# A bottleneck pair on one core: first loads and products in another order, and the last convolutions' seven products moved into the common PSUM pool

## The chip, the cores and the metric

One Trainium2 chip, one of its cores. The metric is the device time of one execution in microseconds (us). The kernel before took 2366.21 us, the median of 4 runs from 2364.62 to 2367.03.

## What is computed

Two residual blocks in a row on x, 16 images of 1024 channels by 32x32 pixels, all in float32:

```python
# layer 0: a bottleneck with local self-attention
h = relu(bn(conv1x1(x, w_conv1)))            # 1024 -> 256
q, k, v = relu(bn(h*wq)), relu(bn(h*wk)), bn(h*wv)
# 3x3 neighbourhoods of k (plus a position table), 32 heads of 8 channels, softmax over 9 taps
h = relu(bn(softmax(q . unfold(k)) . unfold(v)))
x = relu(bn(conv1x1(h, w_conv3)) + x)        # 256 -> 1024
# layer 1: an ordinary bottleneck
h = relu(bn(conv1x1(x, w1)))                 # 1024 -> 256
h = relu(bn(conv3x3(h, w2)))                 # 256 -> 256
x = relu(bn(conv1x1(h, w3)) + x)             # 256 -> 1024
```

## The kernel before, in words

**Tiling.** Channels lie on the 128 partitions, the 1024 pixels of an image on the free axis. A PSUM tile is 128x1024 (two banks of 512); one product is a matmul of 128x128 weights with 128x512 pixels. In float32 the profile shows each product as two MATMUL rows.

**Stages.** The list `stages` names, image by image, the work of TensorE (PE): `conv1` (`first_conv`, L390 through `reduce_part`), `qk` and `v` (`project`, L476, with the position products L522), `fused` (conv3 of layer 0, L422, followed by conv1 of layer 1, L390), `wino` (the 3x3 convolution of four images at once in a Winograd form, `winograd_conv`, L823) and `u3` (the last 1x1 convolution, L422 in `last_sum`). For the last four images (12 to 15) the last convolution is done in another way, `late_sums`: outputs and inputs are split in halves, and a Strassen-like scheme takes seven products in place of eight. `late_weights` makes sums of weights, `change(b)` makes four sums of the image's halves on VectorE (DVE, L1213 to L1220), and a `Pair` handles two output channel blocks with products 1 to 7 (L1252).

**What sets the order.** Nothing is scheduled automatically: the program is written in the order in which each engine runs it, and semaphores hold an instruction until its data and its room are there. The DVE and ScalarE (ACT) work of attention, transforms and weights is drawn into the PE stages word by word from the string `ORDER` (L916): after each part of a stage `Side.passes` takes a word, and its letters run one step of attention (`j`), of its exponentials (`e`), of transforms and weights (`f`), of relays (`m`), ReLU of attended images (`a`), or ReLU of a Winograd image (`w`).

**The start.** `at_first` (L1434) issues loads. `more_weights` (L113) puts weights on SP's DMA queue: the first half of `w1` in two pieces (128 KB, then 384 KB, L131). `more_loads` (L330, DMA at L362) puts x of image 0 on ACT's queue for chunks 0 (two halves) and 1 and on POOL's for chunks 2 to 7. Behind these POOL's queue runs `member_table` (L188, L190), clears `kp` (L1445) and loads the last convolutions' weights (L233). `winograd_weights` turns the 3x3 weights into 36 forms on ACT and DVE (L284 to L294) and writes them to `uw` in HBM (L306); its tiles come from `hpool`, five rooms that it shares with h, q and the attended images.

**The end.** Ahead of `late_sums` the pool `psum` (four 128x1024 tiles) is closed and a pool `banks` opened (four tags of two 128x512 banks). A `Pair` takes two residual tiles r. Its products 1, 6 and 5 add up in one bank, 7 and 4 in another, and DVE adds a bank into the residual in SBUF each time a partial sum is one of the outputs (L1241): 1 to the first half of r0, 6 and 4 to the first half of r1, 7 to the second half of r1, 5 to both second halves. Product 2 has a bank of its own and DVE adds it to r0. Product 3 has a bank into which ACT first copies the second half of r0 (L1237), and from which it copies the sum back (L1276). Then ACT makes both results (L1332: shift, ReLU, pixels put back in order) and POOL sends them (L1333). The last two pairs of image 15 go another way: residual copied to PSUM for both 2 and 3, results straight out of PSUM (L1329), and the very last one in quarters (L1298, L1304, L1305) with its output on SP's and ACT's queues.

## Time and profile before

| | |
|---|---|
| median of 4 runs | 2366.21 us |
| the profiled execution | 2365.78 us, of which the span is 2364.1 us |
| PE busy | 2347.7 us, 99% of the span |
| DVE, ACT, POOL busy | 91%, 39%, 21% |
| HBM traffic | 292 GB/s over the span |
| first product of PE starts | 4.39 us |
| step of two 128x512 MATMULs, all through | 0.43 us |
| last MATMUL starts | 2357.19 us |

PE's busy time is a union of rows that overlap, so "99%" says only that it rarely stood idle. To see a loss on PE one takes the step from one MATMUL's start to the next and compares it with the usual 0.43 us (0.22 us for 256 columns). Summed over the span these steps lose about 15 us; the largest single losses lie at the start, in two Winograd stages (at 678 and 2202 us), between `last_sum` and `late_sums` (2258 us), and at the very end.

### The profile page before, as it was taken

What the parts mean: (1) busy time and instruction counts of PE and PEld (TensorE: products, weight loads), DVE (VectorE), ACT (ScalarE), POOL (GpSimd) and SP (SyncE); (2) the same over time, 40 slices, a digit from 0 to 9 for tenths busy, and PEclk for the clock granted to TensorE, in tenths of its full rate; (3) what the DMA queues carried; (4) which work ended last, traced back from release to release, by engine and by line L of the source; (5) the groups of instructions that cost most, each with busy time, mean ns of one, the idle gap of its engine ahead of it and who ended that gap; (6) DMA issues with size and microseconds to landing.
All of it is one profiled execution on the core that took longest, in us unless ns stands there. A gap on an engine that the chain in (4) does not pass through costs nothing.

```text
span 2364.1 us, 18845 instructions
## 1 busy us (share of the span) xinstructions
PE 2347.7 (99%) x6244; PEld 1138.8 (48%) x6244; DVE 2163.1 (91%) x1786; ACT 931.7 (39%) x890; POOL 490.3 (21%) x900
## 2 busy tenths in 40 slices
PE   9999999999999999999999999999999999999998
PEld 3444444444475444444466444444467444444843
DVE  4999999999999999999989999999989999966687
ACT  3323342324123574433122574324222463444277
POOL 2212121212121332111121232111111231111222
PEclk9999999999999999999999999999999999999999
DMA  9968687978697997687887998688788897699887
GB/s 365 376 210 305 243 288 250 285 274 274 254 354 253 344 387 297 222 263 244 258 313 271 329 388 311 225 276 284 264 296 277 325 371 251 208 353 313 315 295 293
DMA packets 295585, 691.63 MB, mean 293 GB/s; under 512 B 20800, under 2 KB 165184, under 8 KB 286784
## 3 DMA queue, kind: packets, MB, share of 16 engines
q0 software_dynamic: 119888, 471.14, 54.5%
q1 hardware_dynamic: 174944, 218.06, 28.4%
q10 hardware_dynamic: 656, 1.23, 0.1%
q8 instruction: 50, 0.82, 0.1%
q14 instruction: 47, 0.39, 0.1%
HBM read 415.32 MB, written 275.03 MB: 292 GB/s over the span
## 4 chain that ended last, share of the span: by engine, by line
PE 95%; DMA 2%; DVE 2%; ACT 1%; issue 0%; SPq 0%; ACTq 0%; DVEq 0%
PE ps L390 36%; PE ps L422 32%; PE ps L476 13%; PE ps L823 9%; PE ps L1252 4%; DMA U<-uw 1%; DMA uw<-u 1%; DMA g<-in_u2t_dram 1%; PE ps L522 0%; DVE z L849 0%; DVE y L849 0%; ACT kp L489 0%; DVE prod L621 0%; DMA x<-in_x_dram 0%; DVE u L291 0%
## 5 line engine op out<-in xcount | busy, mean ns | idle before, releaser
L390 PE MATMUL ps<-result,u 128*128 128x512 f32 x1024 | 457.8, 592 | 0.0
L422 PE MATMUL ps<-a,w 128*128 128x512 f32 x1024 | 457.7, 592 | 0.0
L390 PE MATMUL ps<-x,w 128*128 128x512 f32 x1024 | 444.3, 594 | 4.5 <-DMA x<-in_x_dram 4.4
L678 DVE TENSOR_TENSOR acc<-e,bnv 128x2048 f32<-128x2048 f32 x144 | 327.5, 2283 | 18.5 <-ACT e L660 15.4
L422 PE MATMUL ps<-y,u 128*128 128x512 f32 x768 | 331.1, 592 | 0.0
L621 DVE TENSOR_TENSOR prod<-qc,bnk 128x2048 f32<-128x2048 f32 x144 | 324.1, 2287 | 1.8
L441 ACT ACTIVATE result<-ps,par 128x1024 f32<-128x1024 f32 x128 | 142.5, 1113 | 457.4 <-PE ps L422 394.0
L390 PEld LDWEIGHTS ps<-x,w 128*128 128x128 f32 x1024 | 195.1, 191 | 250.5 <-issue 242.8
L422 PEld LDWEIGHTS ps<-a,w 128*128 128x128 f32 x1024 | 194.6, 190 | 244.9 <-issue 243.7
L390 PEld LDWEIGHTS ps<-result,u 128*128 128x128 f32 x1024 | 194.4, 190 | 245.1 <-issue 237.8
L696 DVE TENSOR_TENSOR acc<-acc 128x2048 f32<-128x2048 f32 x128 | 293.4, 2292 | 4.4
L422 PEld LDWEIGHTS ps<-y,u 128*128 128x128 f32 x768 | 145.9, 190 | 183.3 <-issue 181.1
L476 PE MATMUL ps<-h,wqk 128*128 128x512 f32 x512 | 222.4, 592 | 0.3 <-ACT h L1091 0.3
L442 POOL DMA_DIRECT2D r<-result x128 | 68.7, 537 | 596.9 <-ACT result L441 592.7
L626 DVE TENSOR_TENSOR prod<-prod 128x2048 f32<-128x2048 f32 (+1 forms) x80 | 166.2, 2077 | 2.3
L476 PEld LDWEIGHTS ps<-h,wqk 128*128 128x128 f32 x512 | 97.1, 190 | 123.2 <-issue 111.2
L441 ACT ACTIVATE result<-ps,bn_sh 128x1024 f32<-128x1024 f32 x96 | 106.8, 1113 | 105.2 <-PE ps L422 102.6
L1091 ACT ACTIVATE h<-ps,par 128x1024 f32<-128x1024 f32 x32 | 38.4, 1203 | 259.7 <-PE ps L390 259.7
L413 ACT ACTIVATE ps<-s 128x1024 f32<-128x1024 f32 x128 | 131.2, 1025 | 15.7 <-DMA s<-in_x_dram 13.2
L489 ACT ACTIVATE kp<-ps,par 128x1024 f32<-128x1024 f32 x64 | 77.3, 1209 | 148.3 <-PE ps L476 116.2
L362 POOL DMA_DIRECT2D x<-in_x_dram x126 | 67.0, 533 | 275.7 <-PE ps L390 206.9
L846 ACT ACTIVATE z<-ps 128x1024 f32<-128x1024 f32 x48 | 49.2, 1024 | 178.7 <-PE ps L823 134.2
(384 smaller groups left out, 2675.3 us busy)
## 6 DMA issues: line engine op xcount, KB each, us to landing
s<-in_x_dram POOLq DMA_DIRECT2D x128, 512.0 KB, 5.9
r<-result POOLq DMA_DIRECT2D x128, 512.0 KB, 4.5
x<-in_x_dram POOLq DMA_DIRECT2D x126, 512.0 KB, 5.2
out_dram<-result POOLq DMA_DIRECT2D x125, 512.0 KB, 6.1
r<-r POOLq DMA_DIRECT2D x111, 512.0 KB, 6.9
v<-v SPq DMA_DIRECT2D x96, 408.0 KB, 4.9
U<-uw SPq DMA_DIRECT2D x60, 512.0 KB, 5.5
bnk<-kp SPq DMA_DIRECT2D x32, 680.0 KB, 7.2
```

What stands on the lines that cost most here:

```text
L390: nc.tensor.matmul(ps[n][:, halves(half)], wt[:, c % (NC // 2), n * P : (n + 1) * P], src[:, halves(half)], start=(c == first), stop=(c == ...
L413: nc.scalar.activation(ps, loaded.pop((self.kind, self.b, o)), AF.Identity)
L422: nc.tensor.matmul(self.ahead[o][:, halves(half)], pieces[key][:, n, o % (NC // 2) * P :][:, :P], self.src[:, n, halves(half)], start=Fals ...
L441: nc.scalar.activation(to_, ps, RELU, bias=self.shift(o), scale=1.0)
L476: nc.tensor.matmul(ps[:, halves(half)], pieces[key][:, m, at : at + P], h[:, m, halves(half)], start=(m == 0), stop=(m == NW - 1),)
L489: nc.scalar.activation(dst, src, func, bias=col(f"L0_conv_{name}_b", n), scale=col(f"L0_conv_{name}_s", n),)
L621: nc.vector.tensor_tensor(by_row(t[:, two]), by_row(qc), kc[:, :, i : i + JROWS, j : j + W], ALU.mult)
L626: nc.vector.tensor_add(u[:, :, 0:4], u[:, :, 0:4], u[:, :, 4:8])
L678: nc.vector.tensor_tensor(by_row(dst), rows(e[:, k, :]).unsqueeze(1).to_broadcast([P, HEAD_DIM, JROWS, W]), vc[:, :, i : i + JROWS, j : j ...
L696: nc.vector.tensor_add(acc, acc, t)
L823: nc.tensor.matmul(acc[i][:, at, :, n, :], pieces[key][:, m, at, n * P : (n + 1) * P], v[:, at, :, m * (TILES + TR) :][:, :, :TILES], star ...
L1252: nc.tensor.matmul(ps, w, by, start=i in (1, 2, 7) and not (i == 2 and self.end), stop=True, skip_group_check=True)
```

## The change

**Start.** A new first step clears 128x256 of a tile with DVE and multiplies it with itself three times on PE (L1461 of the kernel after). `member_table` and the clearing of `kp` stand ahead of all loads on POOL. The first loads are dealt to the queues anew: the first 128 KB of `w1` and x chunks 0 (second half), 1 and 3 on SP, x chunk 0 (first half), the other 384 KB of `w1`'s first half and x chunk 2 on ACT, x chunks 4 to 7 on POOL.

```diff
+    def warm_up():
+        t = apool.tile([P, NPOS, JPIX], F32, tag="pc", name="warm").rearrange("p t w -> p (t w)")
+        nc.vector.memset(t[:, : HALF // 2], 0.0)
+        ps = psum.tile([P, HW], F32, tag="ps", name="ps")
+        for _ in range(3):
+            nc.tensor.matmul(ps[:, : HALF // 2], t[:, :P], t[:, : HALF // 2], start=True, stop=True)
     def at_first():
+        warm_up()
+        member_table()
+        nc.gpsimd.memset(kp, 0.0)
         more_weights()
         more_loads()
...
-        member_table()
-        nc.gpsimd.memset(kp, 0.0)
         load_scaled()
...
-            for part in (slice(0, 1), slice(1, k)) if half == 0 else (slice(0, k),):
-                nc.sync.dma_start(view[:, part], src[:, part])
+            first = 1 if half == 0 else k
+            nc.sync.dma_start(view[:, :first], src[:, :first])
+            if first < k:
+                rest.append((view[:, first:], src[:, first:]))
...
-            by = nc.scalar if loads[0] in (("x", 0, 0), ("x", 0, 1)) else nc.gpsimd
-            for part in (halves(0), halves(1)) if loads[0] == ("x", 0, 0) else (slice(None),):
-                by.dma_start(t[:, part], src[:, part])
+            early = (nc.scalar, nc.sync), (nc.sync,), (nc.scalar,), (nc.sync,)
+            by = early[c] if (kind, b) == ("x", 0) and c < len(early) else (nc.gpsimd,)
+            for at, queue_ in enumerate(by):
+                part = halves(at) if len(by) == 2 else slice(None)
+                queue_.dma_start(t[:, part], src[:, part])
+            if rest:
+                nc.scalar.dma_start(*rest.pop())
```

**Order.** The string `ORDER` is another. Outside the start and the last convolutions most instructions stand as before on every engine. The moves that matter below: on ACT, h of image 0 (L1091 before) stands after one group of weight forms in place of three, and the copy of image 0's position sums (`by_offset`, L530 before) directly behind the second K block, ahead of the forms of the second half of the 3x3 weights; on POOL, in the last Winograd stage, three output transfers stand ahead of the fifth load of transformed pixels instead of behind it.

**Last convolutions.** The pool `psum` stays open to the end, and a `Quad` takes the place of a `Pair`: one 128x1024 tile holds 1, 6, 5 in one bank and 7, 4 in the other; a second tile receives all of r0 from ACT after product 5, products 2 and 3 add to it, and the result comes straight out of it. The order of the products spreads over three quads.

```diff
+        def open(self):
+            self.product(1)
+            self.product(7)
+            self.add(0, 0, 1)
+            self.add(1, 1, 7)
+        def cross(self):
+            self.product(6)
+            self.product(4)
+            self.add(1, 0, 6)
+            self.add(1, 0, 4)
+        def close(self):
+            self.product(5)
+            self.add(0, 1, 5)
+            self.add(1, 1, 5)
+            self.ends = self.room((2,), (3,))
+            nc.scalar.activation(self.ends, self.r[0], AF.Identity)
+            free_late(("r", self.b, 2 * self.q))
+            self.result(1, self.r[1])
+            free_late(("r", self.b, 2 * self.q + 1))
...
     def late_sums():
-        nonlocal banks
-        sums_room.close()
-        banks = ctx.enter_context(tc.tile_pool(name="banks", bufs=2, space=bass.MemoryType.PSUM))
...
+                    this.open()
+                    if before:
+                        before.product(2)
+                    if last_one:
+                        last_one.close()
+                    if before:
+                        before.product(3)
+                        before.result(0, before.ends)
+                    this.cross()
+                    before, last_one = last_one, this
```

The first three quads open before any of them closes (product order 1, 7 of the first, 1, 7 of the second, 6, 4 of the first, 6, 4 of the second, 1, 7 of the third, and so on), and `change(12)` runs three of its four steps ahead of them and the fourth behind the first quad's adds. The last quad has its own order:

```diff
+        def finish(self, before, last_one):
+            self.product(1)
+            self.add(0, 0, 1)
+            before.product(2)
+            last_one.close()
+            before.product(3)
+            before.result(0, before.ends)
+            self.product(6)
+            self.add(1, 0, 6)
+            self.room((7, 4))
+            self.product(7)
+            self.add(1, 1, 7)
+            last_one.product(2)
+            self.product(5)
+            self.split = []
+            for n in range(2):
+                self.add(n, 1, 5)
...
+                if n:
+                    nc.vector.tensor_copy(t, seed)
+                else:
+                    nc.scalar.activation(t, seed, AF.Identity)
+            self.product(4)
+            self.add(1, 0, 4)
+            self.result(1, self.r[1])
+            last_one.product(3)
+            last_one.result(0, last_one.ends)
...
+            for n in range(2):
+                self.product(2, n)
+                self.product(3, n)
...
+                if n == 0:
+                    nc.scalar.activation(to, self.split[n], RELU, bias=self.shift[0], scale=1.0)
+                    nc.sync.dma_start(self.to[0][:, halves(0)], t[:, halves(0)])
+                else:
+                    nc.vector.tensor_scalar(to, self.split[n], self.shift[0], 0.0, ALU.add, ALU.max)
+            nc.scalar.dma_start(self.to[0][: P // 2, halves(1)], t[: P // 2, halves(1)])
+            nc.sync.dma_start(self.to[0][P // 2 :, halves(1)], t[P // 2 :, halves(1)])
```

PE has three products more, those of the cleared tile; of all others it has the same number.

## The prediction

> **What bounds the kernel.** First the shares on the page, then PE's waits, then the timeline where PE loses steps.

> ```profile
> PE 2347.7 (99%) x6244; PEld 1138.8 (48%) x6244; DVE 2163.1 (91%) x1786; ACT 931.7 (39%) x890; POOL 490.3 (21%) x900
> ```
> ```profile
> PE 95%; DMA 2%; DVE 2%; ACT 1%; issue 0%; SPq 0%; ACTq 0%; DVEq 0%
> ```

> The chain that ended last is PE for 95%. The change leaves PE its products, so it can win only what PE loses: about 15 us of lengthened steps, the 4.39 us before the first product and the 6.5 us behind the last. The wait list for PE is short:

> ```profile
> PE ps L390 <- DMA x<-in_x_dram: 4.4, 1, 4.4
> PE ps L823 <- DMA U<-uw: 1.4, 1, 1.4
> PE ps L1252 <- ACT result L441: 1.3, 1, 1.3
> ...
> PE ps L823 <- issue: 0.8, 1, 0.8
> ```

> So 7.9 of 9.8 us waited are four places: first x, a weight load at 678 us, the junction at 2258 us, a load at 2202 us. In the steps the change touches 1.95 us at the start, 0.98 at 33 and 58 us, 1.06 at 2202, 1.72 at the junction and 1.06 at the end, 6.8 in all; the rest of a gain would have to come from the output's way out.

> **a. Cleared products.** Weight loads step with their matmuls:

> ```profile
> 7.11 0.34 PEld L390 LDWEIGHTS ps<-x,w 128*128 128x128 f32 x1 [0.52 <-issue]
> 7.96 0.29 PEld L390 LDWEIGHTS ps<-x,w 128*128 128x128 f32 x1 [0.52 <-issue]
> 8.49 0.19 PEld L390 LDWEIGHTS ps<-x,w 128*128 128x128 f32 x1 [0.24 <-issue]
> 8.92 0.19 PEld L390 LDWEIGHTS ps<-x,w 128*128 128x128 f32 x1 [0.24 <-issue]
> ```

> Starts lie 0.85 us apart until 7.96, then 0.53, then 0.43: half pace until about 8.2 us, 3.8 us after the first product (the window table prints a granted clock of 1.00 there; the steps decide). Five steps lose 0.59 + 3 x 0.42 + 0.10 = 1.95 us. After, DVE clears 128x256 from about 0.8 us (nearest row: DVE on 128x256, 0.42), PE begins near 1.3 and runs six half-pace MATMULs of 256 columns, 6 x 0.43 = 2.6 us, to 3.9: clear of the data at 4.39. If 3.8 us of work count from 1.3, the pace doubles near 5.1; the first long step stays, 3 x 0.42 + 0.10 = 1.37 goes. Ends: 0 (the half microsecond of rest resets it) and 1.95.

> [...]

> **b. Loads.** First products need 128 KB of w1 and 256 KB of x, as before, at the head of the same two queues: 4.39 stays. Chunk 1 is the new deadline: 9.78 us before, 8.3 after with (a). It needs the other 384 KB of w1, now on ACT's queue beside 4 KB rows of x1 and x3 on SP. Before, it landed 4.9 us after issue. DMA moves about 0.39 MB/us (388 to 411 GB/s in the window table); by 3.9 us the first 0.38 MB have moved, and the product follows 0.45 later. With only the 1.15 MB then missing of chunks 0 and 1 the remainder is usable at 3.9 + 2.95 + 0.45 = 7.3 us; with x3 and nearly all of x4 (1.0 MB) in between, at 9.9. I take 8.3, no stall: 0, with the end at +1.5 (all of (a) eaten). POOL's queue loads x4 to x7 about 2.6 us later (0.13 + 0.46 + 2.02, the rows of the members and kp); x4 is due at 18 us, so nothing. The kp clearing, moved ahead, hides in POOL's idle start; w3/u3 follow x as before.

> **c. ACT's order.** h waits behind two groups of forms: PE's step at 33.38 is 0.92 long, the next 0.53, so 0.59 lost. by_offset behind forms that wait for `uw<-u` costs 0.39 at 58.40. Now both stand ahead: -1.0. What is behind: the second group of forms starts 6.2 us later (28.16 to about 34.4), and q of image 0 needs a room that a form's write to HBM frees: it waited 6.8 us for DMA uw<-u, until 46.77, and the position products began at 48.24. Before, that was the third write (issued at about 34.7, 12 us long); now it is the second, issued near 37.3 with one write less ahead of it. Landing by 44 to 45 costs nothing, and this I take; after 12 us again, at 49.3, PE, 2 us earlier, would stall some 3.5. Ends -1.0 and +3.5.

> **d. POOL at 2192 us.**

> ```profile
> 2191.84 0.53 POOL L362 DMA_DIRECT2D V__2_8328<-v  x1 [10.92 <-DMA v<-v]
> 2192.37 1.59 POOL L442 DMA_DIRECT2D out_dram<-result  x3
> 2193.96 0.53 POOL L362 DMA_DIRECT2D V__2_8375<-v  x1
> ```

> POOL waits 10.9 us, sends three outputs, then issues the load for which PE loses 0.98 + 0.08 at 2202. After, the outputs go out during the wait; the load is issued 1.6 us earlier and without 1.5 MB (3.9 us at 0.39 MB/us) ahead of it. -1.0 less 0.2: the outputs now meet the v writes on busy DMA. Ends -1.06, +0.5.

> **e. The junction.**

> ```profile
> 2258.74 1.11 ACT L441 ACTIVATE result<-ps,bn_sh 128x1024 f32<-128x1024 f32 x1
> ```
> ```profile
> 2259.90 1.98 PE L1252 MATMUL ps<-y,u 128*128 128x512 f32 x4 [1.26 <-ACT result L441]
> ```

> Closing a pool makes the first product wait for the last result; steps lose 1.43 + 0.10, and at 2263.9 0.19 more. In a common pool the first quad takes the room of three outputs earlier: free. Then the data decide: y is ready at 2257.6 for product 1 (at 2258.5), the first sum of change at 2259.44 for product 7 (at 2259.4): some 0.3 with the lengthened step. The fourth sum comes behind three sums and two adds, 2258.75 + 6 x 0.65 = 2262.7; product 4, sixth, stands at 2263.0. -1.4; ends -1.7 and 0.

> **f. Steady quads.** Seven products are 7 x 0.86 = 6.0 us. ACT per quad: a copy of 1.0 (L413: 1025 ns) and two results, 4.07 for x2: 5.1 against 0.6 + 0.6 + 4.07 = 5.3 before, and y's ReLU, 2.3, once in four quads. DVE: six adds of 0.65 for seven. The copy into PSUM is ready about 1.9 us after product 5 ends, product 2 uses it 4.3 after. Tiles rotate by four: a quad's first product comes 2.6 us after product 5 of the one two before, whose adds take 1.5. PE covers all: 0. Without that cover (ACT a step late) each quad would lose up to 1 us; ends -0.2 and +2.

> **g. The very end.** From 2346 to 2352 PE loses 1.06 us to DVE adds; the last results are ready 0.9 us after it stops, then 1.5 MB leave:

> ```profile
> 2357.19 0.34 SPq L1330 DMA_DIRECT2D out_dram<-result  x1
> 2357.58 0.42 SPq L1325 DMA_DIRECT2D out_dram<-result  x1
> ```

> After: ACT does copy 1.0, result 2.0, result 2.0, copy 0.6 in a row behind the last quad but one's product 5, and the first quarter products wait about 0.5 for it; DVE's last adds run beside. The last result of ACT is out some 1.6 us after an unstalled PE's end (1.9 before), and half a megabyte leaves on POOL beside SP. -0.5; ends -1.3, +1.0.

> **h. What is kept.** PE arrives 2.4 us earlier from 60 us on. The load of U at 678 us follows K, a product of PE, so its 1.5 us stay; the V loads ahead of it follow DVE, and may keep it late: ends 0 and +1.5, taken at +0.3.

> **Sum.** -1.4 - 1.0 - 0.8 - 1.4 - 0.5 + 0.3 = -4.8 us, on the profiled execution's 2365.78 (span 2364.1 and 1.7 around it): 2361.0. That execution is 0.4 below the median of 4, so the median comes to about **2361.4**. This is a gain of 0.20%; 0.2% (2361.5) is also about what a measurement of this kernel can tell from no change.

> **Rivals.**
> - *The start gives little.* The rest resets the clock, or w1's remainder lands at 9.8: chunk 1 begins as before. For it: 1 KB rows beside 4 KB rows; against: 4.9 us before. 2361.4 + 1.6 = 2363.0.
> - *More than summed.* First step fast too (0.6), d and e whole (0.5), end at -1.2 (0.7): 2359.6.
> - *DVE starts late, slower.* Attention begins at 81.4 us behind the weight forms, which (c) delays by up to 6 us; before, DVE rested 11.3 us at 41 for `uw<-u`, which should absorb it. DVE is 97 to 98% busy from 100 to 600 us and can't catch up. At 309.58 image 1's conv3 starts 3.5 us after ACT's ReLU of its data (306.07), and PE now comes 2.4 earlier. A delay D costs PE D - 3.5 against before, and the 2.4 us gained later stand against it: slower than before from D = 5.9, a microsecond each. With a second lost round of `uw` (some 12 us a write), D = 12: 2366.2 + 6.1 = 2372.3.
> - *q of image 0 late*, as priced in (c): 2361.4 + 3.5 = 2364.9.
> - *The junction stays.* If ReLU and change of y, not the room, ended the wait: 2361.4 + 1.4 = 2362.8.

> **Chances.** Forecast 0.47 (2360.4 to 2362.6, 0.6 of it below 2361.5), little start 0.18, more 0.17, q late 0.07, junction 0.04, DVE late 0.07 (0.05 beyond 0.2%). Faster by over 0.2%: 0.28 + 0.17 = 0.45; slower by over 0.2%: 0.05; between 0.50. Range 2358.8 to 2365.2: it holds the forecast and four rivals with some spread, and leaves out late DVE and the outermost ends, under 0.2 in all.

> **What would show it.** (a) the first block's weight loads 0.43 apart from the second or third on; (b) chunk 1 at 8.3 us without a DMA wait; (c) steps of 0.43 at 33 and 58 us; (d) no PE wait near 2200; (e) no wait on L441; (f) no PE wait between 2262 and 2340; (g) one lengthened step of about 0.5 us in the last 12, and the span's end 6.8 us behind PE's last start (6.9 before). Wrong if conv3 waits for attended data at 309 us, or if quads wait for ACT's copies.

## The result and the profile after

The kernel after took 2369.65 us, the median of 42 runs (2368.11 to 2371.16), against 2366.64 us for the kernel before in 60 runs beside it. The ratio is 1.0010 with a 95% interval of 1.0006 to 1.0015: slower by 0.10%, where 0.20% of gain was forecast. The profiled execution took 2370.43 us, its span 2368.7, 4.6 more than the span before.

The page's first line and PE's waits (time in all, times, longest) of the kernel after:

```profile
PE 2351.2 (99%) x6250; PEld 1141.2 (48%) x6250; DVE 2155.9 (91%) x1771; ACT 929.8 (39%) x872; POOL 490.0 (21%) x899
```
```profile
PE ps L529 <- ACT q L496: 5.5, 1, 5.5
PE ps L1461 <- DVE warm L1458: 1.3, 1, 1.3
PE ps L830 <- DMA V__2_8351<-v: 1.1, 1, 1.1
PE ps L830 <- DMA U<-uw: 1.0, 1, 1.0
...
PE ps L1271 <- ACT ps L1329: 0.5, 1, 0.5
...
PE ps L397 <- DMA x<-in_x_dram: 0.2, 1, 0.2
```

The junction's wait (1.3) is gone from the list. The wait for the first x (4.4) has become one for the cleared tile (1.3) and one of 0.2 for x; the first real product still starts at 4.37 us (4.39 before). A new wait heads the list: the position products of image 0 (L529) wait 5.5 us for ACT's q. The "99%" of the first line does not show it. Two views explain it. The first is ACT's timeline (start, duration, what it does, in brackets the idle time before and what ended it). Two rows of the kernel before, the first weight form and q:

```profile
18.73 0.84 ACT L284 ACTIVATE g<-g 128x768 f32<-128x768 f32 x1 [6.97 <-DMA g<-in_u2t_dram]
46.77 2.30 ACT L489 ACTIVATE q<-ps,par 128x1024 f32<-128x1024 f32 x2 [6.77 <-DMA uw<-u]
```

And of the kernel after, the first row from the view of 0 to 31 us, the others from 30 to 60 us:

```profile
22.73 0.84 ACT L287 ACTIVATE g<-g 128x768 f32<-128x768 f32 x1 [10.21 <-DMA g<-in_u2t_dram]
```
```profile
39.48 0.42 ACT L288 ACTIVATE g<-g 128x256 f32<-128x256 f32 x1 [0.91 <-DVE u L294]
45.66 0.42 ACT L295 ACTIVATE u<-g 128x256 f32<-128x256 f32 x1 [5.77 <-DMA uw<-u]
45.98 0.40 ACT L297 ACTIVATE u<-g 128x256 f32<-128x256 f32 x1
46.29 1.19 ACT L496 ACTIVATE kp<-ps,par 128x1024 f32<-128x1024 f32 x1
51.04 2.30 ACT L496 ACTIVATE q<-ps,par 128x1024 f32<-128x1024 f32 x2 [3.56 <-DMA uw<-u]
```

The reader is to see two things. The first weight form begins at 22.73 us, 4.0 later than before (18.73), because the taps g landed later. And ACT, which runs its list in order, stands twice before q, 5.77 and 3.56 us, each time for a room of `hpool` that a write `uw<-u` has to give back; q begins at 51.04 instead of 46.77.

The second view is the window table of PE's busy time (third field), with the granted clock in the last but two:

```profile
44.00:48.00 4.00, 2.81 (x7) 0.95 (x5) 2.06 (x6) 1.82 (x3) 0.00 (x0) 1.00 1.03 415
48.00:52.00 4.00, 0.00 (x0) 0.00 (x0) 0.31 (x1) 0.96 (x1) 0.00 (x0) 0.84 1.04 411
52.00:56.00 4.00, 3.70 (x17) 0.89 (x18) 1.74 (x5) 3.94 (x8) 1.54 (x2) 0.50 1.06 401
56.00:60.00 4.00, 4.00 (x9) 1.70 (x8) 3.52 (x8) 4.00 (x8) 2.84 (x5) 0.81 1.03 402
```

PE rests, and the clock falls to 0.50 at 50.73 us and is back only at 57.56, in the last row. So the rest costs more than itself: the step across it is 6.1 us, the steps behind are up to 1.0 us long until 57.6, and all together lose 8.2 us, against 0.7 in the same place before (7.6 us more before rounding).

The other places, in steps from start to start: at the start 1.07 us lost (1.96 before); h at 33 us nothing (0.59) and `by_offset` at 58 us nothing beside the halved clock (0.39); the load of U at 684 us 1.28 (1.62); the load of V near 2204 us 1.36 (1.05); the junction and what follows it 0.37 (1.72); the end 0.80 (1.06), and from PE's last start to the end of the span 7.0 (6.9). The first steps, V's load on POOL, and the junction:

```profile
4.37 0.50 PEld L397 LDWEIGHTS ps<-x,w 128*128 128x128 f32 x2 [0.91 <-DMA x<-in_x_dram]
5.38 0.34 PEld L397 LDWEIGHTS ps<-x,w 128*128 128x128 f32 x1 [0.52 <-DMA x<-in_x_dram]
6.24 0.25 PEld L397 LDWEIGHTS ps<-x,w 128*128 128x128 f32 x1 [0.52 <-issue]
6.73 0.19 PEld L397 LDWEIGHTS ps<-x,w 128*128 128x128 f32 x1 [0.24 <-issue]
```
```profile
2200.84 0.53 POOL L367 DMA_DIRECT2D V__2_8351<-v  x1 [7.99 <-DMA v<-v]
```
```profile
2264.48 1.02 PE L1271 MATMUL ps<-y,u 128*128 128x512 f32 x2
2265.50 1.12 PE L1271 MATMUL ps<-bnv,s 128*128 128x512 f32 x2
```

The weight loads are 0.43 apart from 6.73 on (8.49 before). V's load now goes out the moment its data are written, and still comes late. The first Quad's products follow one another with no idle time in brackets.

### The profile page after: what moved, and what is told of

Its sections match the earlier page's. It is cut to its first block, busy times and chain, and to the rows that moved or that the text cites. A ratio compares the mean times of both kernels' runs of the same rounds, so it can differ in the third digit from the quotient of the medians.

```text
span 2368.7 us, 18839 instructions
## 1 busy us (share of the span) xinstructions
PE 2351.2 (99%) x6250; PEld 1141.2 (48%) x6250; DVE 2155.9 (91%) x1771; ACT 929.8 (39%) x872; POOL 490.0 (21%) x899
## 3 DMA queue, kind: packets, MB, share of 16 engines
q10 hardware_dynamic: 912, 1.36, 0.2%
## 4 chain that ended last, share of the span: by engine, by line
PE 93%; DMA 3%; DVE 2%; ACT 1%; issue 0%; ACTq 0%; SPq 0%; DVEq 0%; POOLq 0%
PE ps L397 36%; PE ps L429 31%; PE ps L483 14%; PE ps L830 8%; PE ps L1271 4%; DMA v<-v 1%; DMA g<-in_u2t_dram 1%; DMA U<-uw 1%; PE ps L529 1%; DMA uw<-u 1%; DVE form L759 0%; DVE z L856 0%; DVE y L856 0%; DVE v L759 0%; ACT kp L496 0%; DMA w<-in_w1t_dram 0%
## 5 line engine op out<-in xcount | busy, mean ns | idle before, releaser
L420 ACT ACTIVATE ps<-s 128x1024 f32<-128x1024 f32 x128 | 131.2, 1025 | 15.4 <-DMA s<-in_x_dram 12.9
```

Of the source, the lines that this page charges most:

```text
L420: nc.scalar.activation(ps, loaded.pop((self.kind, self.b, o)), AF.Identity)
```

## The experiments

The theory formed from these views has two parts. Both the new dealing of the loads (g later) and the new opening of `ORDER` (h ahead of two groups of forms) delay the write that frees q's room, and **either alone is enough** to make PE rest (theory A); and the rest then halves PE's clock. The rivals: one of the two causes alone, or something else at the start.

**e1_loads_back** deals the first loads as in the kernel before:

```diff
-            early = (nc.scalar, nc.sync), (nc.sync,), (nc.scalar,), (nc.sync,)
-            by = early[c] if (kind, b) == ("x", 0) and c < len(early) else (nc.gpsimd,)
...
-            if rest:
-                nc.scalar.dma_start(*rest.pop())
+            by = nc.scalar if (kind, b) == ("x", 0) and c < 2 else nc.gpsimd
```

> The kernel after with one thing undone: the first loads are dealt to the queues as in the kernel before. In the kernel after PE rests 5.5 us for q of image 0 at 46.6 us (6.1 us from start to start, 8.2 us of lengthened steps with the slow ones behind it, 0.7 before), and the taps g of the 3x3 weights land 4 us later (ACT's first form at 22.73 in place of 18.73 us). Theory A, two causes, either enough: with g early again the first form's write leaves at 29.5 as before, but the second group of forms still stands behind h on ACT (34.2 us), so the second write, for whose room q waits, still leaves near 36.5 and lands near 49 to 51. PE's rest stays at 3 to 5.5 us: 2366.5 to 2369.7. Rival B, the late g alone: rest gone, 2362 to 2363. Rival C, the order alone: nothing changes, 2369.7, and the first form makes no difference to q.

Measured 1.0000 times the kernel before (0.9991 to 1.0009). g is early (first form at 16.64 us, first write at 27.3), but the second write leaves at 37.14 and q waits for it all the same (ACT's timeline):

```profile
48.18 2.30 ACT L490 ACTIVATE q<-ps,par 128x1024 f32<-128x1024 f32 x2 [6.23 <-DMA uw<-u]
```

PE's rest is 2.3 us, less than the 3 to 5.5 expected, and its clock stays at 1.00 there. So the late g is not the only cause, but a good part of the rest came with it.

**e2_order_back** takes the first 27 words of `ORDER` from the kernel before and leaves the loads:

```diff
-        ". . f . . f . fff . . f . ffffff . . f . . . fj ff ff . jjjf f . j"
+        ". . f . ff . f ff . . f ff ff . . f . fff fj ffff . jj j j . . ."
```

> The kernel after with the other thing undone: the first 27 words of the order string are those of the kernel before (h of image 0 behind three groups of forms, the position sums' copy later), loads as in the kernel after. Theory A: g still lands near 22.7, writes leave at 33.5, 36.2 and 38.8 us, and q waits for the third of them, 12 us, until about 51: PE's rest stays, and h's step (0.6) and the copy's (0.4) come back: 2369 to 2371.5. Rival C, the order alone: 2362.5 to 2363.5. Rival B, late g alone: rest stays, 2370.

Measured 1.0033 (1.0022 to 1.0043), 3 us worse than theory A had it. What it had not seen is that h itself now waits, behind three groups of late forms:

```profile
PE ps L483 <- ACT h L1086: 5.4, 1, 5.4
```

h ends near 40 us, the clock halves for 3.4 us, and q comes at 54.68. In these two profiles the new order is the better one when the taps are late: one and the same product (the 121st MATMUL row behind the cleared ones) starts at 61.59 us here and at 59.93 in the kernel after.

**e3_both_back** joins the two edits.

> Loads and opening order both as in the kernel before; the cleared products, the clearing of kp ahead of the loads, the rest of the order and the last convolutions as in the kernel after. Theory A and rivals B and C alike: first form at 18.7, third write at 34.7, q near 46.8, no rest of PE beyond 0.6, clock kept: the kernel after less 7.5 us, plus 1.0 for h and the copy: 2362.5 to 2363.5. If the rest of 5.5 us comes from elsewhere (the cleared products, the tile they take, kp's clearing): 2369 to 2371.

Measured 0.9982 (0.9973 to 0.9991), on the median of before 2362.4 us. The third write leaves at 32.59 us, q waits for PE alone (41.31), and the window that was empty is full:

```profile
48.00:52.00 4.00, 4.00 (x24) 1.62 (x24) 3.06 (x5) 3.79 (x6) 0.77 (x1) 1.00 1.04 417
```

The four corners are thus: both as after 1.0010, loads back 1.0000, order back 1.0033, both back 0.9982. The same product of PE starts at 59.93, 55.09, 61.59 and 52.63 us in them (53.68 before). Each cause alone delays q and makes PE rest, and both must go for the rest to go, as theory A has it. Their shares are not alike: the late g weighs more, and the two costs do not add up.

What theory A leaves open is why one write lands after 5 us and another after 15. In the traces it goes with whether SP issues the write ahead of POOL's loads of image 1's x or behind the first of them.

```profile
33.72 3.66 POOL L362 DMA_DIRECT2D x<-in_x_dram  x7
```
```profile
32.45 3.69 POOL L367 DMA_DIRECT2D x<-in_x_dram  x7
```
```profile
38.58 3.66 POOL L363 DMA_DIRECT2D x<-in_x_dram  x7
```

(The kernel before, the kernel after, e3.) The writes that are issued before 46 us, in us from issue to landing:

| kernel | first load of image 1's x | writes issued ahead of it | behind it |
|---|---|---|---|
| before | 33.72 | 5.1, 4.4 | 11.9, 14.2, 17.0 |
| after | 32.45 | none | 12.1, 14.2, 14.5 |
| e1 loads back | 35.91 | 5.0 | 11.0, 13.6, 17.1 |
| e2 order back | 32.74 | none | 12.2, 14.9, 15.2 |
| e3 both back | 38.58 | 5.0, 4.6, 6.9, 6.8 | 12.3 |

In all 14 traces of this case the 21 writes ahead took 4.4 to 6.9 us and the 36 behind 10.4 to 17.1. In the kernel after no write is ahead: the change made g 4.0 us later and these loads 1.3 us earlier. No run moved POOL's loads alone, so that they are the cause is read from the times and not tested.

**e11_x1_x3_off_sp** asks which load makes g late:

```diff
-            early = (nc.scalar, nc.sync), (nc.sync,), (nc.scalar,), (nc.sync,)
+            early = (nc.scalar, nc.sync), (nc.scalar,)
```

> The kernel after with x chunk 1 on ACT's queue and chunks 2 and 3 on POOL's, so that of the x loads only half of chunk 0 stands ahead of the taps g on SP. One look, for ACT's first form. If the megabyte of x ahead of g on SP made g late: first form near 17 us (16.6 with the loads as before, 22.7 in the kernel after), and as the order is still the new one, PE's rest at 46 us is 2 to 3 us as with the loads as before. If w1's remainder on ACT or POOL's order made it late: 22 us or so still.

```profile
16.86 0.84 ACT L287 ACTIVATE g<-g 128x768 f32<-128x768 f32 x1 [5.55 <-DMA g<-in_u2t_dram]
```

g is early again: the megabyte of x on SP's queue it was. Up to and with the second piece of g, for which this form waits, that queue is given 2.69 MB in the kernel after and 1.66 MB here. The piece landed at 22.70 and 16.84 us, so the megabyte more took 5.9 us, about 0.17 MB/us, of the 0.39 to 0.41 that all queues together moved in the kernel after from 5 to 25 us (388 to 410 GB/s). As expected q waits on (PE's rest 2.5 us, clock halved for 6.8 us), 2371.42 us in its one run.

**e4_q_room** leaves loads and order, and puts q of image 0 elsewhere:

```diff
-        q = hpool.tile([P, NW, HW], F32, tag="h", name=f"q_{b}")
+        if b == 0:
+            q = apool.tile([P, HEAD_DIM, JPIX], F32, tag="qc", name="q_0").rearrange("p d w -> p (d w)")
+            q = q.rearrange("p (n w) -> p n w", n=NW)
+        else:
+            q = hpool.tile([P, NW, HW], F32, tag="h", name=f"q_{b}")
```

> The kernel after with one tile elsewhere: q of image 0 lies in the room of qc, free at that time, instead of a room of the pool that the forms u share; no wait for a form's write stands before q itself. Theory A: the copy of the first K block still stands behind a form that waits 5.8 us for the first write (45.66), so q begins near 47.5 in place of 51.04, and PE's rest is 2 us in place of 5.5: less 3.5 us, and up to 2.6 more if the slow steps behind the rest (0.85 us apart for 5 us) go with it: 2363.5 to 2366.2. Rival: q's room is not what the rest comes from: 2369.7.

q begins at 47.41 us as expected and PE's rest is 2.0 us, with the clock at half for one window of 3.4 us. By the steps this gains 4.3 us on the kernel after at 60 us. Yet the whole is 1.0003 (0.9994 to 1.0011), 1.7 us better than the kernel after by intervals that overlap. The rest of the gain went at 684 us:

```profile
PE ps L834 <- DMA U<-uw: 3.6, 1, 3.6
PE ps L533 <- ACT q L496: 2.0, 1, 2.0
```

The load of U landed 16.8 us after its issue here and 14.2 in the kernel after, and the longer wait halved the clock a second time (3.4 us from 684.1). The expected 2363.5 to 2366.2 was missed: q's room is what q waited for, as the profile shows, but most of the gain was given back.

**e5_filler** keeps PE busy inside the rest of the kernel after, with five products that are overwritten (added work, no result changes):

```diff
+            for i in range(5 if b == 0 else 0):
+                nc.tensor.matmul(
+                    ps[:, halves(i % 2)], pieces[piece("wqk", 0)][:, 0, :P], h[:, 0, halves(i % 2)],
+                    start=True, stop=True,
+                )
```

> The kernel after with five extra products (128x512, a result that the position products then overwrite) in PE's queue ahead of image 0's position products: they can begin when the first K copy has freed a PSUM tile, near 47.5 us, and keep PE busy until about 51.8, so that of the 5.7 us of rest only two pieces under 1 us stay. The extra work lies inside the rest and delays nothing. Theory: the rest itself halves PE's clock (the record of the kernel after shows the grant at 0.5 for 6.8 us from within the rest): with PE busy the steps behind are 0.43 us again, 2.6 us less at 60 us, and 2367 to 2368.5 in all, some of it lost at the wait for U at 684 us. Rival, the slow steps come from transfers that compete there, or from somewhere else than the rest: steps of 0.85 stay and the time is that of the kernel after, 2369.7.

```profile
48.00:52.00 4.00, 4.00 (x10) 1.72 (x10) 0.64 (x2) 0.57 (x1) 0.00 (x0) 1.00 1.04 413
52.00:56.00 4.00, 3.72 (x21) 0.99 (x20) 1.35 (x4) 3.96 (x7) 1.54 (x2) 1.00 1.06 401
```

Against the same windows of the kernel after the clock stays at 1.00 and the steps behind are 0.43, with the DMA share the same (1.04 and 1.06): the slow steps came from the rest and not from transfers. The whole did not gain (1.0015, 1.0006 to 1.0024): at 684 us PE waited 2.0 us and lost a window of the clock (0.69 from 684 to 688), and a wait for ACT of 1.5 us came up in the last Winograd stage. My 2367 to 2368.5 was wrong; what PE gains ahead of 684 us is not kept by itself.

**e7_early_g_q_room** (e1 and e4 together) and **e8_both_back_q_room** (e3 and e4 together):

> The kernel after with the loads dealt as before and q of image 0 in the room of qc: h still stands ahead of the forms, but neither the late g nor a form's room can hold q. Theory: the first K copy at 40.8, q right behind it, no rest of PE at 46 us, clock kept. What is open is DVE, whose second group of forms still waits for ACT behind h (rest of 7.3 us at 27.7 us) and whose attention begins near 84 in place of 80.5 us: if that shift is carried to 684 us (writes of V from DVE, then the load of U behind them), PE rests there 3 us and its clock halves for a window: 2364 to 2366; if DVE's lateness costs nothing: 2362 to 2363, as with both parts of the start undone.

> Loads and opening order as before, cleared products kept, and q of image 0 in the room of qc, so that the forms have a room more. Theory: nothing waits for q any more, DVE's forms go on earlier (one room more), attention starts at or before 80.5 us: 2361 to 2362.5, the best of these kernels. Rival, q's room is no limit once the first write leaves at 27 to 29 us: the same as without the room, 2362.4.

e7 measured 0.9994 (0.9985 to 1.0003): no rest at 46 us, but h of image 1 came 1.8 us late at 82 us, and the load of U cost 2.6 us and a window of the clock at 681. e8 measured 0.9984 (0.9975 to 0.9993), the same as e3: where the first write leaves at 27 us, and the writes that free q's room leave ahead of POOL's loads, that room is no limit, as the rival had it.

**e6_tail_only** has the start of the kernel before in everything, and the last convolutions and the rest of the order of the kernel after. **e9_no_warm** is e8 without the cleared products, **e10_warm4** is e8 with four in place of three:

```diff
 def at_first():
-        warm_up()
...
-        for _ in range(3):
+        for _ in range(4):
             nc.tensor.matmul(ps[:, : HALF // 2], t[:, :P], t[:, : HALF // 2], start=True, stop=True)
```

> The kernel before at its start in everything (no cleared products, loads, clearing of kp and the first 27 words of the order as before), with the rest of the order and the last convolutions of the kernel after. Theory: the junction's 1.35 us and 0.3 to 0.5 at the end are all that this half of the change brings, and the load at 2200 us is open by 0.5 either way: 1.3 to 2.3 us under the kernel before. Rival, the new last convolutions bring nothing in the whole: within 0.5 of the kernel before. The difference to the run with both parts of the start undone but the cleared products kept is what these products bring, under 1 us by that run's first steps, which stayed 0.85 us apart until 8.3 us.

> The fastest kernel so far (loads and opening order as before, q of image 0 in its own room) without the cleared products. In nine traces the clock's record turns to 1.0 at 8.2 and 10.1 us without these products and between 4.3 and 8.7 us, 5.7 on average, in the seven that have them at 1.25 us (counted without the kernel after: 4.4, 4.3, 8.7, 4.9, 6.3, 5.0, 5.7). Theory, a window that is fixed to the clock and not to the program: first real product near 4.4 us at half pace until 8 to 10 us, so 1 to 2 us slower than with them, 2363.5 to 2366 by the ratio to the kernel before. Rival, the products bring nothing on the whole because the weight load at 677 us lands no earlier: the same within 0.5.

> The same kernel with four cleared products in place of three: at half pace they end near 4.8 us, so that PE does not rest between 3.9 us and the first real product. Theory, a fixed window: the rest of half a microsecond did not matter; the first real product is put off to 4.8 us, the time is the same within 0.5. Rival, the rest empties the window: the steps are 0.43 from 4.8 to 5.5 us on in any execution, 0.5 to 1 us faster.

e6 measured 0.9995 (0.9986 to 1.0003), its span 0.9 us shorter than before: not told from no change, and the 1.3 us expected are inside. e9 and e10 measured 0.9985 (0.9977 to 0.9994) and 0.9982 (0.9973 to 0.9991) beside e8's 0.9984: what the cleared products bring is under what these intervals can tell, some 2 us. In the profiles the first steps are at half pace until 9.8 us in e9 and 5.7 in e8, and the product behind U's load starts at 680.9 and 679.3. e10 shows how such a gain can be spent at once: full pace by 5.1 us, then the next x is late by 2.0 us and the clock halves again.

```profile
8.00:12.00 4.00, 1.99 (x6) 0.72 (x5) 0.00 (x0) 0.00 (x0) 0.56 (x2) 1.00 1.04 403
12.00:16.00 4.00, 4.00 (x7) 1.68 (x6) 2.39 (x15) 0.21 (x1) 0.95 (x2) 0.58 1.03 408
```

The rival, that a rest of half a microsecond empties the window, is not decided by this run. Two other traces speak against it: in e1 and e2 the clock rose at 4.43 and 4.33 us, at the end of a stretch of 3.4 us that has part of that rest in it and was 75% busy.

**e12_after_again** is the kernel after on the chip of e9 to e11.

> The kernel after once more, on this chip, for the distance to the fastest version: 1.001 times the kernel before, rest of 5.5 us at 46 us, its clock at half for one or two windows behind it. If the rest or the number of halved windows differs between executions, the 2.6 us of slow steps are not a constant of the kernel.

Measured 1.0021 (1.0011 to 1.0032): rest 3.7 us, clock halved for 6.8 us at 51.6 and for 3.4 us at 690. So the losses vary between executions, and 1.0010 and 1.0021 are to be read as "slower by 0.1 to 0.2%".

Where the time is decided, from one profile each (span's end less the start of the product that waits for U near 684 us; in e6, e9 and e12 the record names another release for it, which came 0.1 to 0.8 us behind U):

| kernel | that product starts | from there to the end | clock halved there |
|---|---|---|---|
| before | 680.1 | 1684.0 | no |
| after | 685.8 | 1682.9 | no |
| e1 loads back | 683.8 | 1683.7 | yes |
| e2 order back | 689.2 | 1684.3 | yes |
| e3 both back | 679.4 | 1682.2 | no |
| e4 q's room | 684.0 | 1684.0 | yes |
| e5 filler | 685.1 | 1684.9 | yes |
| e6 tail only | 680.7 | 1682.4 | no |
| e7 loads back, q's room | 680.7 | 1683.9 | yes |
| e8 both back, q's room | 679.3 | 1682.8 | no |
| e9 as e8, no cleared products | 680.9 | 1684.1 | yes |
| e10 as e8, four cleared products | 682.1 | 1681.6 | no |
| e11 x1 and x3 off SP | 687.6 | 1682.1 | no |
| e12 after again | 688.7 | 1683.9 | yes |

The second column spreads over 10 us, the third over 3.3, about half of which is the halved window (some 1.7 us). So most of what the kernels differ in is settled before 690 us. Where no window is halved, the part behind is 1.1 to 2.4 us shorter than before (1684.0 less 1681.6 to 1682.9), and the start of the kernel after costs 5.7 (685.8 less 680.1).

## Why the prediction was wrong, step by step

- **What bounds the kernel** was read rightly: PE, and what it loses in steps. But I looked for new losses only where the change had old ones.
- **a, cleared products, -1.4**: 0.9 gained in the profiled run, within its ends. Over the traces full pace begins between 4.3 and 10.6 us with them and at 8.2 to 10.1 without. That the rest at 3.9 us resets the clock, as the end at 0 had it, no run shows by itself: in the kernel after the clock rose at 6.36 us, behind 3.41 us that hold this whole rest (3.98 to 4.37 us) and in which PE was busy for 84%; in e3 it rose at 8.7. On the whole time the intervals of e8 and e9 do not tell it from nothing.
- **b, loads, 0**: this step failed. It priced the deadline of chunk 1, which was met (no wait from 6.2 us on), and x chunk 4 on POOL's queue. The other user of SP's queue, the taps g, now behind the loads of x, was not in the list. They came 4.0 us later: the x loads on SP cost 5.9 (e11 against the kernel after), and the clearing of kp ahead of POOL's loads, which puts these off, gave some 2 to 3 back (18.87 in e6 without it, 16.14 in e9 with it).
- **c, ACT's order, -1.0**: this step failed with it. The two stalls went (0.59 and 0.39, right to the hundredth), but "landing by 44 to 45 costs nothing, and this I take" did not come true. The write left at 36.80, close to the 37.3 assumed, and landed 14.2 us later, at 51. The prediction took the 12 us of the write issued at 34.75 as the worst; the same trace had 14.2 us for the one issued at 37.84, the nearest to 37.3. "One write less ahead of it" did not count: the write stood behind POOL's loads of image 1's x, as all writes now did. The price was also too low, twice: a second wait of 5.8 us for the write before it stands in front of q, and the halved clock adds 2.6. +7.6 us measured, +3.5 as the far end.
- The rival **q of image 0 late** was thus the right mechanism with 0.07 of chance and less than half its price. With 7.6 for 3.5 it would have stood at 2369.0; 2369.65 was measured. That this is so near is in part luck: a, d and g came out 2.0 us worse than put in and h 0.6 better, and the profiled execution, from which these steps are read, lies 0.8 above the median.
- **d, POOL at 2192, -0.8**: +0.3. The load is issued where the data allow, at 2200.84, after 8.0 us of waiting for `v<-v`. In the other runs the steps there lose from nothing (e10) to 1.8 us (e5, where the wait is for ACT's z). The order was not what ended last.
- **e, the junction, -1.4**: -1.35. **f, steady quads, 0**: no wait of PE between 2266 and 2352 us. Both right.
- **g, the very end, -0.5**: -0.26 in the steps, +0.15 behind them. The size was wrong; the wait for ACT's last copy, 0.5, stood where it was put.
- **h, what is kept, +0.3**: never came up in the kernel after, since PE arrived late. In the kernels that arrive early the step across the load of U (e3, e6 to e10) loses 1.9 to 2.8 us instead of 1.6, and two of the six have a halved clock behind it, so its end of +1.5 was nearer.
- **DVE late** did not happen: attention begins at 82.3 us (81.4 before) and conv3 of image 1 has 4.5 us of slack.

The sum of the steps as measured is -0.9 (a) - 1.0 + 7.6 (c, which b made) - 0.3 + 0.3 - 1.35 - 0.1 = +4.25 of the 4.6 us between the two spans.

The best kernels here are e3, e8, e9 and e10, 0.9982 to 0.9985 of the kernel before and not told from each other. They have the new end, the old loads and the old opening order, and the clearing of kp ahead of POOL's loads. That clearing makes g earlier and POOL's loads of image 1's x later (37.9 to 38.6 us; 34.4 in e6, which leaves it where it was). e6 has 0.9995, and the intervals overlap.

## What to carry to other kernels

When a load is put ahead on a queue, list everything that is already on that queue and follow each of them to its first user and to the rooms that user gives back, not only the transfer that was meant to gain. Where a landing time decides, take the duration that the trace shows for that transfer in that traffic, and see which other queue's loads it will meet: here that was the difference between 5 and 15 us. Price a rest of PE with the half pace that may follow: waits of 2.0 us cost a halved window in e4, e5 and e10, waits of 2.1 and 2.6 us cost none in e3 and e8. And where two reorderings may delay the same release, undo each alone and both together: here undoing one took PE's rest from 5.5 to 2.3 us, undoing the other made the kernel slower (1.0033 for 1.0010), and only both together removed it.
